# A projection by W.T in seven half-width products per pair of row blocks, with the right-hand sums of the next layer finished by accumulating DMAs

## The chip, the cores and the metric

The kernel runs on one core of one Trainium2 chip. The time is that of one execution on the device, in microseconds (us), and the median of several executions is compared. A profile of a single execution gives the time of every instruction: PE is TensorE (matmuls), PEld its weight loads, DVE VectorE, ACT ScalarE, POOL GpSimd, SP SyncE.

## The reference

There are N = 4096 nodes with D = 512 features. `adj` is a 4096 x 4096 matrix, W is 512 x 512, all in float32.

```
# layer 0
inc = adj + (adj > 0) / max(sqrt(row sum of (adj > 0)), EPS)
x1  = layernorm(x + (inc @ x) / (row sum of inc))

# layer 1
A2     = adj + I
dscale = diagonal(A2) ** -0.5
temp   = A2 @ x1 @ W.T
out    = layernorm(x1 + relu(dscale[:, None] * A2 * dscale[None, :] @ temp))
```

So layer 1 is two products by A2 (the program calls them k = 2 and k = 3), with a projection by W.T and a scaling of the rows by dscale in between.

## The kernel before, in words

**Strassen's scheme, two levels deep.** A product of two matrices that are cut into four quarters each needs seven products of quarters instead of eight, in Winograd's form, with sums of quarters on the left (S1 to S4), on the right (T1 to T4) and on the result. The kernel does this twice. The outer level cuts A2 and x1 into quarters: its seven products are numbered p = 1 to 7. Each outer product is again cut in four, and its seven inner products run as seven 512-column matmuls per 128 rows of the inner dimension, each into a PSUM bank of its own. The eighth bank, `spare()`, is for everything else.

**The steps.** `steps` lists (k, s, p, kk). For each k the result's columns are handled in two strips, s = 0 and 1, each strip does its outer products p in the order 4, 5, 1, 6, 7, 2, 3 (k = 2) or 2, 3, 5, 1, 6, 7, 4 (k = 3), and each outer product takes eight steps kk = 0 to 7 of seven matmuls (`multiply2`, L250). That makes 224 steps. Layer 0 runs before them in its own loop, with one level of the scheme (L455).

**What VectorE does for a step.** `prepare(n)` (L216) forms the four left-hand sums of step n (`add_up`, L166 to L169); in p = 1 and 2 for kk below 4, and in p = 6 and 3 for kk from 4 on, it also adds a tile of A2 to a resident tile r (L232 and L224, 2048 elements per partition). `sum_b` (L245 to L247) forms the right-hand sums of two steps. Everything is issued in the order of the program text, engine by engine: step n's code first prepares step n + 2, then issues the matmuls of step n, then the rest. The tiles for the sums are three in turn, so `prepare(n + 2)` can begin when TensorE has read the sums of step n - 1.

**What happens after eight steps.** `outer` (L682) combines the seven banks, through `inner` (L661: two copies by ScalarE, seven VectorE instructions of 512 elements), either straight into one of the four result quarters c11, c12, c21, c22 (`into`), or through a tile y that is then added to quarters (`by_way`). What remains to be added between whole quarters is put into the list `deferred`, and each later step takes one entry of it, after its `prepare` and `sum_b` and ahead of its matmuls. For k = 2 the lower half of the result (c21, c22; h = 1) is complete after p = 7, the upper half (c11, c12; h = 0) after p = 3.

**The projection.** When a half of a strip is complete, its eight row blocks of 128 rows are put into `queue`, and steps kk = 1 to 5 take one each, after their own seven matmuls. `project` (L733) multiplies the row block by W.T in four 512-column matmuls that add up in the spare bank (L740); ScalarE scales the rows by dscale on the way out (L743). The right-hand operands of k = 3 lie in DRAM (the tiles `ob`): B11, B21, B22 and the sums T1 to T4. The lower half is written as B21 and B22 (L745). For the upper half the matching lower block is read back (L748), B11 is written (L749), and one step later VectorE forms T1 to T4 in `outer_sums` (L127 to L133) and they are written (L754). In k = 3 SP loads these operands again (L238). The DMAs of the projection are issued on GpSimd's queue (POOL).

The first steps of p = 2 and p = 3 (h = 1), and of p = 4 and p = 5 of the next strip (h = 0; for the last strip, p = 2 and p = 3 of k = 3) are where the projection is interleaved.

Of the kernel before, what the change touches and what calls it, by code (L numbers as in the profile page):

```python
# [26 lines left out]
def tile_adj_resnorm_d2(  # L27
# [56 lines left out]
    small = ctx.enter_context(tc.tile_pool(name="small", bufs=6))  # L84
# [107 lines left out]
    queue, later, deferred = [], [], []  # L192
# [57 lines left out]
    def multiply2(n, acc, between=None):  # L250
        k, s, p, kk = steps[n]
        a, sm = ready.pop(n)
        b, t = (y[n // 2][:, kk % 2] for y in (raw_b, sums_b))
        for m, (right, left) in enumerate((
            (a[:, A11, :], b[:, 0, :]), (a[:, A12, :], b[:, 2, :]), (sm[:, S2, :], t[:, 2, :]),
            (sm[:, S1, :], t[:, 0, :]), (sm[:, S3, :], t[:, 1, :]), (sm[:, S4, :], b[:, 3, :]),
            (a[:, A22, :], t[:, 3, :]),
        )):
            if m == 3 and between is not None:
                between()  # L260
            nc.tensor.matmul(acc[m], left, right, start=(kk == 0), stop=(kk == NQ - 1))  # L261
# [101 lines left out]
    def spread(j, part):  # L363

        if part == 0:
            n = small.tile([P, 2], F32, name="n")
# [104 lines left out]
    def take(h, acc):  # L471

        y = row_tile("z", 4)
# [5 lines left out]
    def combine(acc):  # L479

        q1, q2, q6, q5, q7, q3, q4 = acc
        top, low = row_tile("z", 4), row_tile("z", 4)
        p1, p5 = row_tile("p1", 1)[:, 0:W], row_tile("p5", 1)[:, 0:W]
        u2, u3 = row_tile("u2", 1)[:, 0:H], row_tile("u3", 1)[:, 0:H]
        deg = small.tile([P, 2], F32, name="deg")
# [19 lines left out]
    def layer0(j, C):  # L505

        rd = small.tile([P, 2], F32, name="rd")
# [28 lines left out]
    deg0 = small.tile([P, 2], F32, name="deg")  # L536
# [118 lines left out]
    wt = accs.tile([P, ND, D], F32, name="wt")  # L655
# [26 lines left out]
    def outer(k, p, acc):  # L682
# [13 lines left out]
        if k == 2:  # L696
# [6 lines left out]
            elif p == 7:  # L703
                def then(i, y):
                    nc.vector.tensor_sub(c21[:, i, :], c21[:, i, :], y)
                    less(c22[:, i, :], y, c12[:, i, :])
                by_way(then)
            else:
                dst = {2: c11, 3: c12}[p]
                by_way(lambda i, y: add(dst[:, i, :], y))  # L710
# [22 lines left out]
    def project(h, item):  # L733

        j, r, cols = item
        b = j + h * NP
        pv = spare()
        for f in range(2):
            for e in range(2):
                nc.tensor.matmul(pv, C_of[2][h][f][:, 2 * r + e, cols], wt[:, 2 * f + e, :],  # L740
                                 start=(f + e == 0), stop=(f + e == 2))
        z = row_tile("z", 4)
        nc.scalar.activation(z, pv, AF.Copy, scale=dscale[:, b:b + 1])  # L743
        if h:
            nc.gpsimd.dma_start(out=in_outer(3, j, slice(B21, B22 + 1)), in_=split(z))  # L745
            return
        low = split(row_tile("z", 4))
        nc.gpsimd.dma_start(out=low, in_=in_outer(3, j, slice(B21, B22 + 1)))  # L748
        nc.gpsimd.dma_start(out=in_outer(3, j, slice(B11, B11 + 1)), in_=z[:, 0:H].unsqueeze(1))  # L749

        def rest():
            t = row_tile("t", 1, (P, 4, H))
            outer_sums(t, z[:, 0:H], z[:, H:D], low[:, 0, :], low[:, 1, :])
            nc.gpsimd.dma_start(out=in_outer(3, j, slice(T1, T4 + 1)), in_=t)  # L754
        later.append(rest)
# [10 lines left out]
    def fetch(kind, h, *items):  # L766

        for j, _, _ in items if kind is not project else ():
# [80 lines left out]
    for n, (k, s, p, kk) in enumerate(steps):  # L849
# [11 lines left out]
        if deferred:  # L861
            deferred.pop(0)()
        multiply2(n, acc, (lambda: take_up(items.pop(0))) if len(items) > 1 else None)
        if n == 0:
            layer0(NP - 1, C)
        elif n == 1:
            operands(NP - 1, C)
            nc.gpsimd.dma_start(out=wt, in_=w_t.rearrange("(a p) o -> p a o", p=P))
# [4 lines left out]
        for rest in held:  # L873
            rest()
        if 1 <= kk <= (6 if end else 5):
            for kind, args in queue[:2]:
                fetch(kind, *args)
        if kk == NQ - 1:
            outer(k, p, acc)
            if (k, p) in DONE:  # L880
                h = DONE[k, p]
                if n + 1 < len(steps):
                    queue.extend(((project, layer1)[k - 2], (h, b)) for b in blocks(h, s))
# [50 lines left out]
```

## Time and profile before

| | us |
|---|---|
| median of 3 runs | 2297.93 (2297.89 to 2298.2) |
| the profiled execution | 2296.9 |
| its span, first to last instruction | 2295.1 |
| TensorE busy | 2269.1 |
| VectorE busy | 1799.6 |
| ScalarE busy | 349.0 |
| GpSimd busy | 235.0 |

The granted TensorE clock is 0.996 of full speed. The products of k = 2 and 3 begin at about 804 us and last to the end. A line of the profile's groups has the source line, the engine, the operation, the tiles (out<-in), the shape and the count, then the busy time, the mean duration of one in ns, and the idle time of the engine just before the group with what ended it. A line of the chain of waits in order of time has its start, its length, and what ran. A line of the timeline has start, length, engine, line and operation; what stands in brackets at its end is the time the engine was idle before it, and who ended that. A line of the waits has who waited for whom, the sum in us, how often, and the longest. An f32 matmul appears as two records.

### The profile page before, as it was taken

The numbers are of one execution on the slowest core, as the hardware profiler recorded it, in microseconds if no ns is written. First come the engines' busy times: TensorE is split into PE (matmuls) and PEld (weight loads), VectorE is DVE, ScalarE is ACT, GpSimd is POOL, SyncE is SP. The second block draws the span as 40 slices with busy tenths as digits, with TensorE's granted clock in tenths as the row PEclk, the third lists the DMA queues.
The fourth block names the chain that finished last, engine by engine and source line by source line (L and its number), as shares of the span: only waits on it lengthen the run. The fifth ranks groups of instructions, "written<-read, shape, count | busy, mean of one in ns | idle before, by whom it ended". The sixth has DMA issues, their size and how long they took to land.

```text
span 2295.1 us, 20944 instructions
## 1 busy us (share of the span) xinstructions
PE 2269.1 (99%) x7166; PEld 1345.7 (59%) x7167; DVE 1799.6 (78%) x2563; ACT 349.0 (15%) x802; POOL 235.0 (10%) x384
## 2 busy tenths in 40 slices
PE   8999999999999999999999999999999999999997
PEld 6888888888888844444444444444444444444443
DVE  6988898988988777787666778666567788767787
ACT  4333233332231000000000000000000011200013
POOL 0111111211122100000101100010100000100010
PEclk9999999999999999999999999999999999999998
DMA  9788778877776576474665856476665676766672
GB/s 328 276 283 264 253 233 275 271 263 260 250 246 230 205 269 258 187 271 178 241 242 227 299 190 247 161 284 255 236 237 212 227 247 240 261 242 216 222 257 105
DMA packets 149482, 553.64 MB, mean 241 GB/s; under 512 B 16592, under 2 KB 24800, under 8 KB 110976
## 3 DMA queue, kind: packets, MB, share of 16 engines
q1 hardware_dynamic: 114624, 417.38, 51.4%
q0 software_dynamic: 34752, 134.93, 16.5%
q8 instruction: 57, 0.93, 0.2%
q14 instruction: 49, 0.40, 0.0%
HBM read 438.98 MB, written 113.26 MB: 241 GB/s over the span
## 4 chain that ended last, share of the span: by engine, by line
PE 91%; DVE 3%; DMA 3%; issue 2%; ACT 0%; POOL 0%; SPq 0%; ACTq 0%; DVEq 0%; POOLq 0%
PE q L261 56%; PE q L455 27%; PE q L740 5%; PE q L468 2%; DMA nat<-adj 1%; DMA a<-adj_r 1%; PE q L760 1%; DVE s L166 0%; DVE a L425 0%; DMA ob<-t 0%; DVE mask L418 0%; DVE r L232 0%; ACT nat L315 0%; DMA sc<-n 0%; DVE s L168 0%
## 5 line engine op out<-in xcount | busy, mean ns | idle before, releaser
L261 PE MATMUL q<-s,ts 128*128 128x512 f32 x1344 | 614.0, 592 | 0.3 <-DVE u L667 0.2
L455 PE MATMUL q<-b,s 128*128 128x256 f32 (+1 forms) x1920 | 454.4, 379 | 0.0
L261 PEld LDWEIGHTS q<-s,ts 128*128 128x128 f32 x1344 | 255.0, 190 | 321.0 <-issue 293.2
L166 DVE TENSOR_TENSOR s<-a 128x1024 f32<-128x1024 f32 x236 | 288.6, 1223 | 167.9 <-PE q L261 132.9
L455 PEld LDWEIGHTS q<-b,s 128*128 128x128 f32 x1920 | 363.1, 189 | 53.1 <-DVE z L493 0.5
L455 PE MATMUL q<-b,a 128*128 128x258 f32 (+1 forms) x1440 | 352.5, 380 | 1.1 <-ACT p L486 1.1
L261 PE MATMUL q<-a,tr 128*128 128x512 f32 x704 | 331.2, 592 | 1.5 <-DMA a<-adj_r 1.4
L455 PEld LDWEIGHTS q<-b,a 128*128 128x128 f32 x1440 | 272.5, 189 | 41.2 <-ACT p L486 1.9
L261 PE MATMUL q<-s,tr 128*128 128x512 f32 x448 | 228.7, 592 | 0.0
L261 PEld LDWEIGHTS q<-a,tr 128*128 128x128 f32 x704 | 131.6, 190 | 158.2 <-issue 153.1
L315 ACT ACTIVATE nat<-nat,tiny 128x512 f32<-128x512 f32 x240 | 170.9, 714 | 239.1 <-DMA nat<-adj 238.9
L261 PE MATMUL q<-a,ts 128*128 128x512 f32 x352 | 180.1, 593 | 0.8 <-DVE y L672 0.8
L169 DVE TENSOR_TENSOR s<-a,s 128x512 f32<-128x512 f32 x236 | 163.3, 692 | 8.0
L168 DVE TENSOR_TENSOR s<-a,s 128x512 f32<-128x512 f32 x236 | 163.2, 692 | 8.1
L418 DVE SCALAR_TENSOR_TENSOR mask<-a,sc 128x1024 f32<-128x1024 f32 (+2 forms) x129 | 154.0, 1195 | 2.1
L425 DVE TENSOR_TENSOR a<-a,mask 128x1024 f32<-128x1024 f32 x123 | 150.7, 1225 | 6.2
L261 PEld LDWEIGHTS q<-s,tr 128*128 128x128 f32 x448 | 85.1, 190 | 107.2 <-issue 100.9
L665 ACT COPY p<-q 128x512 f32<-128x512 f32 x28 | 16.3, 584 | 742.7 <-PE q L261 742.7
L261 PEld LDWEIGHTS q<-a,ts 128*128 128x128 f32 x352 | 66.6, 190 | 85.9 <-issue 77.7
L740 PE MATMUL q<-wt,c 128*128 128x512 f32 x256 | 115.1, 592 | 0.0
L166 DVE TENSOR_TENSOR s<-r 128x1024 f32<-128x1024 f32 x48 | 58.7, 1222 | 57.1 <-PE q L261 51.1
L261 PE MATMUL q<-r,tr 128*128 128x512 f32 x192 | 90.2, 592 | 0.0
(141 smaller groups left out, 1645.1 us busy)
## 6 DMA issues: line engine op xcount, KB each, us to landing
a<-adj_r SPq DMA_DIRECT2D x112, 1024.0 KB, 5.8
a<-oa SPq DMA_DIRECT2D x80, 1024.0 KB, 5.2
nat<-adj SPq DMA_DIRECT2D x240, 256.0 KB, 7.5
a<-adj_q SPq DMA_DIRECT2D x60, 1024.0 KB, 6.3
tr<-ob SPq DMA_DIRECT2D x112, 512.0 KB, 3.9
oa<-sr POOLq DMA_DIRECT2D x64, 512.0 KB, 7.5
oa<-r POOLq DMA_DIRECT2D x32, 1024.0 KB, 6.1
y<-x POOLq DMA_DIRECT2D x64, 256.0 KB, 6.5
```

What stands on the lines that cost most here:

```text
L166: nc.vector.tensor_add(s[:, S3:S1 + 1, :], a[:, A11:A22 + 1, :], a[:, A21, :].unsqueeze(1).to_broadcast([P, 2, w]))
L168: nc.vector.tensor_add(s[:, S2, :], a[:, A11, :], s[:, S1, :])
L169: nc.vector.tensor_add(s[:, S4, :], a[:, A12, :], s[:, S2, :])
L261: nc.tensor.matmul(acc[m], left, right, start=(kk == 0), stop=(kk == NQ - 1))
L315: nc.scalar.activation(y, a, AF.Sign, bias=tiny, scale=2.0 ** 64, accum_out=accum)
L418: nc.vector.scalar_tensor_tensor(m, v, 0.0, s.unsqueeze(1).to_broadcast(list(v.shape)), op0=ALU.is_gt, op1=ALU.mult)
L425: nc.vector.tensor_add(z, z, y)
L455: nc.tensor.matmul(acc[m][:, 0:w], left, b[:, right, 0:w], start=(kk == 0), stop=(kk == NP - 1))
L468: nc.tensor.matmul(y[:, 0:w], left, slots[kk][:, op, 0:w], start=(kk == 0 and left is k1), stop=(kk == NP - 1 and left is k2))
L665: nc.scalar.copy(p1, q1)
L740: nc.tensor.matmul(pv, C_of[2][h][f][:, 2 * r + e, cols], wt[:, 2 * f + e, :], start=(f + e == 0), stop=(f + e == 2))
L760: nc.tensor.transpose(ps[:, at + i * P:at + (i + 1) * P], C_of[3][h][d // 2][:, 2 * r + d % 2, cols], ident)
```

## The change

W.T is kept as seven right-hand operands of 128 x 2 x 256, three of its quarters and the four sums T1 to T4: four DMAs in step 1 load the quarters (the fourth, B12, into the place of T4), and `outer_sums` forms the four sums in step 4. The projection takes two row blocks at a time, r = 0 and 1 of the same n, as the two row halves of a left operand whose two column halves are the two quarters of the result. Seven products of two 256-column matmuls each go through the spare bank, one after the other, spread over three steps: three in kk = 1 (or 4), three in kk = 2 (or 5), one in kk = 3 (or 6), each placed between the seven matmuls of its step, after the first, the third and the fifth. ScalarE copies each product to one half of the tiles p1, p5, u2, u3. VectorE forms the four left-hand sums behind the first step, and combines the seven copies behind the third.

The combined blocks are scaled in place by ScalarE. The lower half (h = 1) writes B21 and B22 and starts T2, T3 and T4 with its own parts; the upper half (h = 0) writes B11 and T1 and adds its parts of T2, T3 and T4 in DRAM by DMAs that accumulate. The lower block is no longer read back, and `outer_sums` is no longer run for these blocks.

After p = 7 of k = 2 the banks are combined straight into c22, and c21 and c22 get their remaining sums by two entries of `deferred` over whole quarters; while pairs are waiting for the projection, a step takes all entries of `deferred`. The list `pairs` takes the place of `queue` for k = 2.

To make room, the pool `small` has 5 buffers instead of 6, the tile z 2 instead of 4 (in layer 0 as well), and the tiles n, deg and rd 2.

```diff
@@ multiply2
-    def multiply2(n, acc, between=None):
+    def multiply2(n, acc, between):
...
-            if m == 3 and between is not None:
-                between()
+            if m in between:
+                between[m]()
             nc.tensor.matmul(acc[m], left, right, start=(kk == 0), stop=(kk == NQ - 1))
@@ -652,7 +652,8 @@
     quarters = [[accs.tile([P, 4, SW], F32, name=f"c{h}{f}") for f in range(2)] for h in range(2)]
 
     C_of = {2: quarters, 3: quarters[::-1]}
-    wt = accs.tile([P, ND, D], F32, name="wt")
+
+    wt = accs.tile([P, 7, 2, H], F32, name="wt")
     pools["turn"] = [ring, ring, ringx, ring]
     scope = ExitStack()
     pools["resident"] = scope.enter_context(tc.tile_pool(name="resident", bufs=1))
@@ -701,10 +702,8 @@
                 deferred.extend((lambda: add(c12, c11), lambda: nc.vector.tensor_sub(c21, c21, c12),
                                  lambda: add(c12, c22)))
             elif p == 7:
-                def then(i, y):
-                    nc.vector.tensor_sub(c21[:, i, :], c21[:, i, :], y)
-                    less(c22[:, i, :], y, c12[:, i, :])
-                by_way(then)
+                into(c22)
+                deferred.extend((lambda: nc.vector.tensor_sub(c21, c21, c22), lambda: less(c22, c22, c12)))
             else:
                 dst = {2: c11, 3: c12}[p]
                 by_way(lambda i, y: add(dst[:, i, :], y))
@@ -730,29 +729,73 @@
 
         return [(r * NQ + s * SB + n, r, slice(n * P, (n + 1) * P)) for n in range(SB) for r in range(2)]
 
-    def project(h, item):
-
-        j, r, cols = item
+    def project(h, s, n):
+
+
+        cols = slice(n * P, (n + 1) * P)
+        a11, a12, a21, a22 = (C_of[2][h][f][:, 2 * r:2 * r + 2, cols] for r in range(2) for f in range(2))
+        places = [t[:, i * H:(i + 1) * H] for t in (row_tile(t, 1) for t in ("p1", "p5", "u2", "u3")) for i in range(2)]
+        q = []
+
+        def product(left, right):
+            def now():
+                ps = spare()[:, 0:H]
+                for e in range(2):
+                    nc.tensor.matmul(ps, left[:, e, :], wt[:, right, e, :], start=(e == 0), stop=(e == 1))
+                q.append(places[len(q)])
+                nc.scalar.copy(q[-1], ps)
+            return now
+
+        yield {1: product(a11, B11), 3: product(a12, B21), 5: product(a22, T4)}
+        s1, s2, s3, s4 = (y[:, 2 * i:2 * i + 2, :] for y in (row_tile("y", 2, (P, 4, P)) for _ in range(2)) for i in range(2))
+        nc.vector.tensor_add(s1, a21, a22)
+        nc.vector.tensor_add(s2, a11, s1)
+        nc.vector.tensor_add(s3, a11, a21)
+        nc.vector.tensor_add(s4, a12, s2)
+        yield
+        yield {1: product(s2, T2), 3: product(s3, T3), 5: product(s1, T1)}
+        yield
+        yield {1: product(s4, B22)}
+        q1, q2, q4, q6, q7, q5, q3 = q
+        z = [row_tile("z", 2) for _ in range(2)]
+        nc.vector.tensor_add(z[0][:, 0:H], q2, q1)
+        nc.vector.tensor_add(q6, q6, q1)
+        nc.vector.tensor_add(q7, q7, q6)
+        nc.vector.tensor_add(q6, q6, q5)
+        nc.vector.tensor_add(z[0][:, H:D], q3, q6)
+        nc.vector.tensor_sub(z[1][:, 0:H], q4, q7)
+        nc.vector.scalar_tensor_tensor(z[1][:, H:D], q7, -1.0, q5, op0=ALU.mult, op1=ALU.subtract)
+        t = row_tile("t", 1, (P, 4, H))
+        for r in range(2):
+            j = r * NQ + s * SB + n
+            leave_operands(h, j, z[r], t[:, 2 * r, :], t[:, 2 * r + 1, :])
+        yield
+
+    def leave_operands(h, j, z, t, m):
+
+
         b = j + h * NP
-        pv = spare()
-        for f in range(2):
-            for e in range(2):
-                nc.tensor.matmul(pv, C_of[2][h][f][:, 2 * r + e, cols], wt[:, 2 * f + e, :],
-                                 start=(f + e == 0), stop=(f + e == 2))
-        z = row_tile("z", 4)
-        nc.scalar.activation(z, pv, AF.Copy, scale=dscale[:, b:b + 1])
+        nc.scalar.activation(z, z, AF.Copy, scale=dscale[:, b:b + 1])
+        first, second = z[:, 0:H], z[:, H:D]
+        nc.vector.tensor_sub(t, first, second)
+
+        def put(op, y, **how):
+            nc.gpsimd.dma_start(out=in_outer(3, j, slice(op, op + 1)), in_=y.unsqueeze(1), **how)
+
         if h:
+            nc.scalar.mul(m, second, -1.0)
             nc.gpsimd.dma_start(out=in_outer(3, j, slice(B21, B22 + 1)), in_=split(z))
-            return
-        low = split(row_tile("z", 4))
-        nc.gpsimd.dma_start(out=low, in_=in_outer(3, j, slice(B21, B22 + 1)))
-        nc.gpsimd.dma_start(out=in_outer(3, j, slice(B11, B11 + 1)), in_=z[:, 0:H].unsqueeze(1))
-
-        def rest():
-            t = row_tile("t", 1, (P, 4, H))
-            outer_sums(t, z[:, 0:H], z[:, H:D], low[:, 0, :], low[:, 1, :])
-            nc.gpsimd.dma_start(out=in_outer(3, j, slice(T1, T4 + 1)), in_=t)
-        later.append(rest)
+            put(T2, m)
+            put(T3, second)
+            put(T4, t)
+        else:
+            nc.vector.tensor_sub(m, second, first)
+            put(B11, first)
+            put(T1, t)
+            nc.scalar.mul(second, second, -1.0)
+            put(T2, m, accum_op=ALU.add)
+            put(T3, second, accum_op=ALU.add)
+            put(T4, m, accum_op=ALU.add)
 
     def turn_back(ps, at, h, r, cols, fs):
 
@@ -858,20 +901,34 @@
         items = [queue.pop(0) for _ in range(min(len(queue), 2 if end else 1))] if 1 <= kk <= (6 if end else 5) else []
         held = later[:]
         later.clear()
-        if deferred:
+        while deferred:
             deferred.pop(0)()
-        multiply2(n, acc, (lambda: take_up(items.pop(0))) if len(items) > 1 else None)
+            if not pairs:
+                break
+        between = {3: lambda: take_up(items.pop(0))} if len(items) > 1 else {}
+        if 1 <= kk <= 6:
+            if kk % 3 == 1:
+                pair = project(*pairs.pop(0)) if pairs else None
+            if pair is not None:
+                between = next(pair)
+        multiply2(n, acc, between)
         if n == 0:
             layer0(NP - 1, C)
         elif n == 1:
             operands(NP - 1, C)
-            nc.gpsimd.dma_start(out=wt, in_=w_t.rearrange("(a p) o -> p a o", p=P))
+            parts = w_t.rearrange("(f e p) (o d) -> f o p e d", e=2, p=P, o=2)
+            for op, (f, o) in {B11: (0, 0), T4: (0, 1), B21: (1, 0), B22: (1, 1)}.items():
+                nc.gpsimd.dma_start(out=wt[:, op], in_=parts[f, o])
+        elif n == 4:
+            outer_sums(wt[:, T1:T4 + 1], wt[:, B11], wt[:, T4], wt[:, B21], wt[:, B22])
         if n % 2 == 1:
             load_b_up_to(n // 2 + 3)
         for item in items:
             take_up(item)
         for rest in held:
             rest()
+        if 1 <= kk <= 6 and pair is not None:
+            next(pair)
         if 1 <= kk <= (6 if end else 5):
             for kind, args in queue[:2]:
                 fetch(kind, *args)
@@ -879,8 +936,10 @@
             outer(k, p, acc)
             if (k, p) in DONE:
                 h = DONE[k, p]
-                if n + 1 < len(steps):
-                    queue.extend(((project, layer1)[k - 2], (h, b)) for b in blocks(h, s))
+                if k == 2:
+                    pairs.extend((h, s, i) for i in range(SB))
+                elif n + 1 < len(steps):
+                    queue.extend((layer1, (h, b)) for b in blocks(h, s))
             if n == len(steps) - 1 - NQ:
                 last = sorted(blocks(1, s), key=lambda b: b[1])
                 queue.extend((layer1_first, (1, *last[i:i + 2])) for i in range(0, len(last), 2))
```

More of the change, by code (lines that the diff above doesn't have):

```diff
@@ L83, in tile_adj_resnorm_d2 @@
     const = ctx.enter_context(tc.tile_pool(name="const", bufs=1))
-    small = ctx.enter_context(tc.tile_pool(name="small", bufs=6))
+    small = ctx.enter_context(tc.tile_pool(name="small", bufs=5))
     psum = ctx.enter_context(tc.tile_pool(name="psum", bufs=1, space=bass.MemoryType.PSUM))
@@ L191, in tile_adj_resnorm_d2 @@
     made = {"a": 0, "s": 0, "load": 0, "load_b": 0}
-    queue, later, deferred = [], [], []
+    queue, pairs, later, deferred = [], [], [], []
     def fresh():
@@ L365, in spread @@
         if part == 0:
-            n = small.tile([P, 2], F32, name="n")
+            n = w1_pool.tile([P, 2], F32, name="n", bufs=2)
             nc.vector.tensor_reduce(n, counts.pop(j), axis=mybir.AxisListType.X, op=ALU.add)
@@ L471, in take @@
     def take(h, acc):
-        y = row_tile("z", 4)
+        y = row_tile("z", 2)
         nc.scalar.copy(y[:, 0:H], acc[0][:, 0:H])
@@ L481, in combine @@
         q1, q2, q6, q5, q7, q3, q4 = acc
-        top, low = row_tile("z", 4), row_tile("z", 4)
+        top, low = row_tile("z", 2), row_tile("z", 2)
         p1, p5 = row_tile("p1", 1)[:, 0:W], row_tile("p5", 1)[:, 0:W]
         u2, u3 = row_tile("u2", 1)[:, 0:H], row_tile("u3", 1)[:, 0:H]
-        deg = small.tile([P, 2], F32, name="deg")
+        deg = small.tile([P, 2], F32, name="deg", bufs=2)
         nc.scalar.copy(p1, q1[:, 0:W])
@@ L505, in layer0 @@
     def layer0(j, C):
-        rd = small.tile([P, 2], F32, name="rd")
+        rd = small.tile([P, 2], F32, name="rd", bufs=2)
         nc.vector.reciprocal(rd, C[2])
@@ L535, in tile_adj_resnorm_d2 @@
     scale[0] = w1_pool.tile([P, 2, P], F32, name="sc")
-    deg0 = small.tile([P, 2], F32, name="deg")
+    deg0 = small.tile([P, 2], F32, name="deg", bufs=2)
     def load_half(h, c):
@@ L766, in fetch @@
     def fetch(kind, h, *items):
-        for j, _, _ in items if kind is not project else ():
+        for j, _, _ in items:
             b = j + h * NP
```

## The prediction

> **What bounds the kernel now.** I read the busy shares first, then the chain in order of time, then the order of VectorE's instructions where the projection begins.
>
> ```profile
> PE 2269.1 (99%) x7166; PEld 1345.7 (59%) x7167; DVE 1799.6 (78%) x2563; ACT 349.0 (15%) x802; POOL 235.0 (10%) x384
> L740 PE MATMUL q<-wt,c 128*128 128x512 f32 x256 | 115.1, 592 | 0.0
> DVE t L127 <- DMA ob<-t: 64.9, 12, 8.0
> ```
>
> TensorE is busy 99% of the span, and before L740 it never waits. VectorE waits 64.9 us for the T DMA (third line), yet TensorE waits for nothing then: that idle time costs nothing. Matmul records overlap (a mean of 592 ns for half of an f32 matmul), so I take durations from the chain, which is in order:
>
> ```profile
> 59.49 13.87 PE q L468 x64
> ...
> 1068.01 3.43 PE q L740 x8
> 1071.44 6.01 PE q L261 x14
> ```
>
> One step of seven 512-column matmuls takes 6.01 us, 0.858 each; one projected row block (four such) 3.43 us; 32 matmuls of 256 and 258 columns 13.87 us, 0.433 each. So TensorE work saved is time saved, as long as VectorE keeps up. Whether it does is seen at the hand-over from p=7 to p=2 (s=0):
>
> ```profile
> 1044.45 0.68 DVE L666 TENSOR_TENSOR y<-q,p 128x512 f32<-128x512 f32 x1
> ...
> 1045.96 1.88 PE L261 MATMUL q<-a,tr 128*128 128x512 f32 x4
> ...
> 1051.43 1.12 PE L261 MATMUL q<-a,ts 128*128 128x512 f32 x2 [0.16 <-DVE y L672]
> ...
> 1054.55 1.22 DVE L166 TENSOR_TENSOR s<-a 128x1024 f32<-128x1024 f32 x1
> ...
> 1057.14 2.28 DVE L232 TENSOR_TENSOR r<-r,a 128x2048 f32<-128x2048 f32 x1
> ...
> 1058.40 3.60 PE L740 MATMUL q<-wt,c 128*128 128x512 f32 x8
> ...
> 1059.34 0.68 DVE L245 TENSOR_TENSOR ts<-tr 128x512 f32<-128x512 f32 x1
> ...
> 1060.86 1.22 DVE L166 TENSOR_TENSOR s<-a 128x1024 f32<-128x1024 f32 x1
> ```
>
> TensorE starts p=2 at 1045.96 while VectorE works without a gap until past 1060: it combines p=7's banks from 1044.45 to 1054.55, then prepares. TensorE lives on two prepared steps. Start to start, VectorE's pieces cost: a `prepare` 2.59 us, its add to r 2.20, the right-hand sums 1.52. A combination straight into a quarter costs 4.78:
>
> ```profile
> 1293.97 0.68 DVE L666 TENSOR_TENSOR c<-q,p 128x512 f32<-128x512 f32 x1
> ...
> 1298.75 1.22 DVE L166 TENSOR_TENSOR s<-a 128x1024 f32<-128x1024 f32 x1
> ```
>
> [...]
>
> **The change, part by part.**
>
> *Products.* Two row blocks cost 2 × 3.43 = 6.87 us before. Seven products are 14 matmuls of 256 columns: 14 × 0.433 = 6.07. Sixteen pairs: 109.9 − 97.1 = **−12.8 us**. It would be nothing if such a matmul took 0.49. Between two products lie two 512-column matmuls, 1.72 us; the copy out of the bank needs 0.37 (ScalarE's 256-column copy in the layer-0 rows), so one bank is enough.
>
> *The hand-over, p=7 to p=2.* The combination no longer changes c21 and c22 on the way; two whole-quarter instructions do it afterwards, queued on VectorE behind the `prepare` of kk=2 and the sums. Both must end before the first products, which now stand after the first matmul of kk=1 and no longer behind all seven. VectorE: 1044.45 + 4.78 + 2.59 + 2.20 + 1.52 + 2.28 (a 2048-element add) = 1057.82 for c21, 1060.1 for c22. TensorE: kk=0 lasts until 1051.97, the first matmul of kk=1 until 1052.83; then it must wait for c21 and start again (0.16, as above), until 1057.98: 5.15 us. The second product waits 0.13 for c22. Behind that VectorE has prepare and r of kk=3 (until 1064.84) and the pair's sums; the second is ready at 1065.72, TensorE asks at 1065.42: 0.46 with the restart. Together 5.74. The wait at 1051.43 goes (0.42, against a steady 6.01): +5.3. In s=1 the combination starts at 1437.56, and I place TensorE's start at 1438.64: 6.17, less 0.86 saved, +5.3. **+10.6 us**.
>
> *VectorE in p=2 and p=3 of k=2 (h=1).* A pair costs four sums (1.48, as L127 to L133 take 1.47), then seven adds, the scaling on ScalarE and an add behind each scaling: 2.73 plus two chained scalings (0.75 estimated, between L743's 0.69 and L161's 0.81), the negation of m between (0.4) and a last add: 4.6. From the release that lets the seventh prepare of p=2 run to the second sum of the fourth pair (p=3, kk=5) VectorE never rests: seven prepares 18.1, three adds to r 6.6, four right-hand sums 6.1, p=2's combination by way 7.7, two pairs' endings 9.2, three and a half half-pairs' sums 2.5 with the restart: 50.2. TensorE needs 0.86 + 6.44 + 2 × 6.01 + 2 × 7.31 + 6.44 + 7.31 + 0.86 = 48.55 (kk with three products 7.31, with one 6.44). So it waits 1.65, in both s: **+3.3 us**, bounds 0 and 7 (an error of 0.5 in each ending makes 1.0 per s, of 2% in the rest as much). Queued behind these adds is every later `prepare`, so nothing is made up within the group. At the end of p=2 the next banks come free 0.6 us before they are asked for: nothing.
>
> *h=0 pairs* (p=4, p=5, and p=2, p=3 of k=3). VectorE has no adds to r there; an ending is 5.9 with two more adds. It fits between the releases: 0, bounds 0 and 3.
>
> *DMAs.* Per pair 8 (h=1) or 10 (h=0) of 128 or 256 KB on POOL's queue, before 2 or 6; POOL is 10% busy and an issue takes 0.55 to 0.72. No engine but VectorE waits for them: z and t have only room for one pair, so the next pair's ending needs the last DMA landed. It has some 16 us; ten issues take 6, a plain 128 KB DMA lands in 5.4 at the median: hidden. An accumulating one is not shown. Bounds: as the plain one, or the 12.7 of the slowest store into ob. I take about 8, within the 16. A gain from it is excluded, since TensorE waits for no DMA there now. SP's loads of the operands come more than 15 us after the last store: 0.
>
> *Layer 0 with two z buffers:* the next combination comes 20 us after the last store is issued (539.88 against 560.25): 0. *W's four loads and its T sums* (2.8 us of VectorE near 842) shift prepares that are some 2 us early: 0 to 1. *`small` with 5 buffers, deferred in a loop elsewhere:* 0.
>
> Sum: −12.8 + 10.6 + 3.3 = +1.1. The profiled execution took 2296.9 (span 2295.1), 1.0 below the median of the runs, 2297.93. So 2298.0 for its like and **2299.0** for the median.
>
> **Rivals.**
> *The accumulating DMAs are late (slower).* At p=4 to p=5 VectorE starts the combination at most 1 us ahead of need. If a DMA takes 12.7 and only eight are under way at once, the tenth lands after 1.2 + 12.7 + 12.7 = 26.6, 10 later than allowed; TensorE then loses some 9 in each of p=4 and p=5, less in k=3: 2299 + 18 = 2317. It decides from 8 us per DMA on. For it: the slowest store; against: the median.
> *VectorE's endings are dearer (slower).* With 6.0 instead of 4.6 the lag in p=3 grows by 2.8 per s and p=2's bank slack is gone: some 6 more, 2305. For it: the chain between VectorE and ScalarE, twice per ending, is not shown; against: DVE's wait for ACT z at L127 is short (L743's end to L127's start 0.03).
> *The hand-over is hidden (faster).* If VectorE were a step earlier, the 10.6 would go: 2288. Against: the start at 1044.45 follows work without a gap from the release on, in both s.
> *256-column matmuls between 512-column ones cost more*, say 0.49: no gain, 2312. Against: L455 keeps 0.434 over 1232 matmuls.
>
> **How the numbers follow.** A measurement can tell about 0.2%, 4.6 us, from no change: 2293.3 to 2302.5. My forecast's own range is 2295 to 2303; 0.50. Dearer endings 0.20, late DMAs 0.12, the matmul case 0.04: slower 0.36. Hidden hand-over 0.14, in part at least. The range for 8 in 10 leaves out the DMA and matmul cases and a hand-over that is wholly hidden: 2292 to 2309.
>
> **What would show it.** L744 at 0.43 a matmul and some 97 us in all; waits of TensorE for c21's subtraction, twice, 5 us each, after the first matmul of p=2's kk=1; waits of 1 to 3 us for y in p=3's kk=5; no wait of DVE on ob DMAs beyond a few us. No wait at the hand-over, or VectorE waiting on ob for tens of us, would prove me wrong.

## The result, and the profile after

The changed kernel took 2304.97 us at the median of 10 executions (2301.77 to 2307.82). The kernel before, run beside it, took 2300.91 us at the median of 10 (2297.89 to 2302.57). The medians differ by 4.1 us; the ratio is 1.0020, with a 95% interval of 1.0011 to 1.0029, which is slower by some 4.6 us, just at the edge of what can be told from no change. The forecast was 2299.0 us, in a range of 2292 to 2309: +1.1 us. The result lies in that range, and outside the narrower one of 2295 to 2303.

The small sum hides large terms. First the page after, with the engines' busy times and the groups of the new line L744 (line, engine, operation, tiles, shape and count, then busy time, mean ns, idle time before and what ended it):

```profile
PE 2261.5 (98%) x7359; PEld 1384.0 (60%) x7359; DVE 1860.6 (81%) x2715; ACT 403.6 (18%) x946; POOL 291.5 (13%) x467
L744 PE MATMUL q<-wt,y 128*128 128x256 f32 x256 | 65.7, 379 | 0.0
L744 PE MATMUL q<-wt,c 128*128 128x256 f32 x192 | 51.7, 393 | 12.8 <-DVE c L706 12.8
```

TensorE has less to do than before: 2261.5 us. But its products with c as the left operand waited 12.8 us for VectorE's L706, the subtraction that makes c21. The longest waits of TensorE in k = 2 and 3 (who waited for whom, sum, times, longest):

```profile
PE q L744 <- DVE c L706: 12.8, 2, 6.4
PE q L261 <- DVE c L667: 3.6, 3, 3.0
PE q L803 <- DVE c L726: 3.3, 3, 1.3
```

The third wait was there before as well (3.1 us). The second is new: 3.0 us at once, at the change from p = 5 to p = 1 in s = 1. The chain of waits at the hand-over from p = 7 to p = 2 (s = 0), in order of time (start, length, what):

```profile
1044.37 2.28 DVE r L232
1046.65 0.60 DVE c L667
...
1051.43 1.15 DVE s L166
...
1054.02 2.20 DVE r L232
1056.22 0.61 DVE ts L245
...
1057.74 2.21 DVE c L706
1059.95 0.04 issue
1060.00 2.08 PE q L744 x4
1062.07 3.41 PE q L261 x4
1065.49 1.16 PE q L744 x4
```

Two things are to be seen. The subtraction of c21 comes last of a long row on VectorE, in which two adds to r (L232) of 2.28 and 2.20 us stand, those of kk=1 and kk=2 of p=2. And after the wait the matmuls are slow: four of L261 take 3.41 us, 0.85 a record, where 0.43 is the rule. The busy times by stretch say why; the column ahead of the DMA share is the granted TensorE clock:

```profile
1046.00:1053.00 7.00, 6.72 (x17) 2.76 (x15) 6.65 (x10) 0.00 (x0) 0.00 (x0) 1.00 0.59 224
1053.00:1060.00 7.00, 0.58 (x3) 0.00 (x1) 6.86 (x8) 0.00 (x0) 0.00 (x0) 0.69 0.41 151
1060.00:1063.00 3.00, 3.00 (x6) 2.13 (x7) 3.00 (x2) 0.37 (x1) 0.00 (x0) 0.50 0.01 3
1063.00:1066.00 3.00, 3.00 (x5) 1.36 (x5) 2.93 (x4) 0.00 (x0) 0.00 (x0) 0.51 0.00 0
1066.00:1069.00 3.00, 3.00 (x11) 1.89 (x11) 2.49 (x5) 0.37 (x1) 0.00 (x0) 1.00 0.00 0
```

TensorE stands still for 6.4 us, and for some 6 us after that its clock is half. PE counts as fully busy in those 6 us, so the busy shares don't show the loss.

To add the losses up, I take every matmul record of k = 2 and 3 and count what its distance to the next exceeds 0.429 us (512 columns) or 0.216 us (256 columns). I call that the excess; it holds waits and slow stretches alike. The last 16 records of the program, of 128 columns, are not in it.

| excess, us | before | after |
|---|---|---|
| p=7 to p=2, s=0 | 0.4 | 10.2 |
| p=7 to p=2, s=1 | 1.3 | 9.9 |
| p=5 to p=1, s=1 | 0.4 | 5.0 |
| k=2 and 3 in all | 4.3 | 27.1 |

So 22.8 us more is lost. The length of k = 2 and 3, from the first matmul of L261 to the last matmul of all, went from 1479.2 to 1487.6 us, 8.4 more. The last 16 records took 1.2 us less than before, which leaves 13.2 us for what the products save; the forecast was 12.8. The spans of the profiled executions differ by 9.7 (2304.8 against 2295.1). Layer 0 took 788.1 us in the profile before and 788.4 after, and 786.6 to 791.6 over all the profiles. This scatter is larger than the difference of the medians, so below I quote the length of k = 2 and 3, taken from one profiled execution of each kernel, beside the medians.

### The profile page after: what moved, and what is told of

Read it like the earlier page. It is cut to its first block, busy times and chain, and to the rows that moved or that the text cites. A ratio compares the mean times of both kernels' runs of the same rounds, so it can differ in the third digit from the quotient of the medians.

```text
span 2304.8 us, 21997 instructions
## 1 busy us (share of the span) xinstructions
PE 2261.5 (98%) x7359; PEld 1384.0 (60%) x7359; DVE 1860.6 (81%) x2715; ACT 403.6 (18%) x946; POOL 291.5 (13%) x467
## 4 chain that ended last, share of the span: by engine, by line
PE 94%; DVE 3%; DMA 2%; issue 0%; ACT 0%; SPq 0%; ACTq 0%; DVEq 0%
PE q L261 56%; PE q L455 31%; PE q L744 4%; PE q L468 2%; DMA a<-adj_r 1%; DVE r L232 1%; PE q L803 1%; DMA nat<-adj 0%; DVE s L166 0%; DMA s<-adj_q 0%; DMA a<-adj_q 0%; DVE s L168 0%; DVE c L706 0%; ACT nat L315 0%; DVE st L868 0%
## 5 line engine op out<-in xcount | busy, mean ns | idle before, releaser
L261 PE MATMUL q<-s,ts 128*128 128x512 f32 x1344 | 622.3, 595 | 0.1
L261 PEld LDWEIGHTS q<-s,ts 128*128 128x128 f32 x1344 | 256.3, 191 | 308.9 <-issue 281.0
L261 PE MATMUL q<-a,tr 128*128 128x512 f32 x704 | 338.8, 596 | 4.9 <-DVE c L667 3.6
L261 PE MATMUL q<-s,tr 128*128 128x512 f32 x448 | 228.8, 592 | 0.0
L261 PEld LDWEIGHTS q<-a,tr 128*128 128x128 f32 x704 | 132.1, 191 | 149.7 <-issue 136.2
L261 PE MATMUL q<-a,ts 128*128 128x512 f32 x352 | 179.8, 592 | 0.0
L261 PEld LDWEIGHTS q<-s,tr 128*128 128x128 f32 x448 | 85.1, 190 | 93.5 <-issue 83.7
L261 PEld LDWEIGHTS q<-a,ts 128*128 128x128 f32 x352 | 66.8, 190 | 84.4 <-issue 77.7
L408 POOL DMA_DIRECT2D oa<-sr x64 | 57.9, 904 | 283.7 <-DVE sr L399 181.4
L261 PE MATMUL q<-r,tr 128*128 128x512 f32 x192 | 93.2, 592 | 0.0
```

The costliest lines, as they stand in the source:

```text
L408: nc.gpsimd.dma_start(out=dst, in_=sr.rearrange("p m (k i) -> p (m k) i", i=P))
```

## The experiments

### The kernel before, a second time

There is no edit; it is the same kernel on the chip of the next three.

> The kernel before, unchanged, for its trace beside the others of this call. Two readings of the hand-over from p=7 to p=2: if VectorE's wait of 2.0 us for the load of p=2's second tile (seen in the trace after, in both strips) belongs to the chip or the day, it is here too, and the combination of p=7's banks starts some 2 us later against TensorE than in the trace of before, with TensorE waiting 1.5 to 3 us in each strip for the seventh bank. If it belongs to the change, VectorE waits 0 to 0.9 us for it here, as before. Time 2298 to 2301.

It took 2297.37 us; k = 2 and 3 took 1477.0 us with an excess of 3.4, against 1479.2 and 4.3 in the first profile. So a length can be relied on to about 2 us. VectorE did not wait for the load of p=2, kk=1, where the changed kernel had waited 2.0 us in s=0 and 2.1 in s=1. But the three changed kernels that follow, profiled on the same chip, waited 0 to 0.9 us for it too, so this run does not tie that wait to the change.

### Seven fillers in place of the wait

```diff
+                for _ in range(fill):
+                    nc.tensor.matmul(spare(), ident, wt[:, B11].rearrange("p e d -> p (e d)"), start=True, stop=True)
...
-        yield {1: product(a11, B11), 3: product(a12, B21), 5: product(a22, T4)}
+        yield {1: product(a11, B11, 7 if h and n == 0 else 0), 3: product(a12, B21), 5: product(a22, T4)}
```

> The changed kernel with seven 512-column matmuls (6.0 us, results not used) put into the spare bank in front of the first product of the lower half, in both strips, where TensorE waits 6.6 us for c21. Theory one (the wait also halves TensorE's clock: after it, ten to fifteen matmuls ran at half rate, 3.0 to 3.2 us more in each strip): TensorE doesn't idle, the clock stays at 1.0, the wait becomes work of the same length, and the time falls by about 6 us against the changed kernel: 2299 where that is 2305. Rival (those microseconds are further waits for VectorE and not the clock): the same time as the changed kernel within 1 us, or up to 1 us more.

2303.53 us (17 executions), ratio 1.0025 (1.0018 to 1.0032); k = 2 and 3: 1485.6 us, 2.0 less than after, where theory one gave 6. No stretch of half clock followed the hand-over. But a filler stood 1.18 us from the next, not 0.86, so seven lasted until 1063.2, 2.9 us past c21's end at 1060.34. The run shows the clock, not the saving; that was left to four fillers, below.

### c21 and c22 by way of y again

```diff
-                into(c22)
-                deferred.extend((lambda: nc.vector.tensor_sub(c21, c21, c22), lambda: less(c22, c22, c12)))
+                def then(i, y):
+                    nc.vector.tensor_sub(c21[:, i, :], c21[:, i, :], y)
+                    less(c22[:, i, :], y, c12[:, i, :])
+                by_way(then)
```

> The changed kernel with the sums of c21 and c22 formed on the way again, bank by bank, as in the kernel before; all else of the change stays. Theory one (what costs is that the two whole-quarter sums stand behind a prepare, its add to r and the right-hand sums): c21 is ready with the combination, 10.1 us after its start and not 13.4; TensorE waits about 2 us for the seventh bank and 1 to 2 for c21 in place of 6.6[...]; 6 to 7 us less per strip, so about 2292 where the changed kernel has 2305. Rival (VectorE's volume up to the pair's sums decides, whatever the order): the wait only moves to the sums y in kk=2, and the time falls by 1 to 3 us.

2303.2 us (11 executions), ratio 1.0022 (1.0013 to 1.0031). The first waits of this run:

```profile
PE q L746 <- DVE y L754: 9.3, 2, 4.7
PE q L805 <- DVE c L728: 3.3, 3, 1.3
```

The wait for c21 is gone, and one for the pair's sums y, one step later, stands in its place in each strip, 4.8 us of excess with half clock behind it. k = 2 and 3 took 1483.9 us. That is the rival's account, and not theory one's.

### The deferred sums, c21 and c22, ahead of the next step's work

```diff
         load_up_to(n + LA + PF)
+        while pairs and deferred:
+            deferred.pop(0)()
         if n + LA < len(steps):
...
-        while deferred:
-            deferred.pop(0)()
-            if not pairs:
-                break
+        if deferred:
+            deferred.pop(0)()
```

> The changed kernel with the two whole-quarter sums ahead of the prepare in p=2's first step, instead of behind it, its add to r and the right-hand sums. Same volume of work, another order. Theory one (only the order costs): no wait for c21 any more, 2305 falls by 15 to 20 us to about 2287. Rival (VectorE's volume decides): c21 is in time, but the second sum of the pair's left operands stays where it was, about 21.3 us after the combination starts, and TensorE, now earlier, waits for it in kk=2 for 5 to 6 us, with the clock halved after it: within 3 us of the changed kernel.

2300.55 us (21 executions), ratio 1.0012 (1.0006 to 1.0019); k = 2 and 3: 1482.1 us. Its first wait:

```profile
PE q L744 <- DVE y L752: 9.7, 2, 5.3
```

c21 was in time, and again y was late, by as much as before. These two runs say that the order within VectorE's row only moves the wait: between the last product of p=7 and the first pair's sums there is more work on VectorE than TensorE gives it time for. An add to r still stood ahead of the pair's sums in both: what is moved ahead here are the entries of `deferred`.

### Adds to r two steps later

The add to r of step n had been issued in `prepare(n)`, two steps before TensorE reads that step. It is moved behind the pair's work of step n.

```diff
-        if k == 2 and p in (1, 2) and kk < EARLY:
-            nc.vector.tensor_add(r, r, a)
         ready[n] = a, sm
...
+        a_now = ready[n][0]
         multiply2(n, acc, between)
...
             next(pair)
+        if k == 2 and p in (1, 2) and kk < EARLY:
+            add(resident[kk], a_now)
```

> The adds to r of the first two strips of p=1 and p=2 (k=2, kk under 4) are issued two steps later, when their block is used, and after the pair's work of that step; nothing else differs from the changed kernel. Theory A (the VectorE work ahead of a new first use sets both waits: the combination of p=5 starts late because the pair's ending and two adds to r stand before it, and in p=2 an add to r stands before the sums): the wait of about 3.2 us at p=5 to p=1 and its stretch of half clock vanish (excess there from 5.0 to under 1 us); the hand-over of p=7 to p=2 shortens by the 1.3 us of an add to r at most, since the wait for c21 is not behind it. About 5 us under the changed kernel, some 2299 to 2300 us. Theory B (the wait at p=5 to p=1 comes from the bank's reading alone, whatever stands before it): no change, 2304 us. Theory C (the adds are only moved to where they delay the next use): a new wait of 2 to 3 us elsewhere, 2303 to 2305 us.

2288.87 us (5 executions), ratio to the kernel before 0.9964 (0.9952 to 0.9977): faster than both. The gain over the changed kernel is far above what I expected: 16.7 us in k = 2 and 3 (1471.0), some 13 by the ratios. I had allowed 1.3 us at the hand-over. The timeline of TensorE there (start, length, engine, line, operation; in brackets the idle time before) shows why:

```profile
1051.94 1.02 PE L259 MATMUL q<-a,tr 128*128 128x512 f32 x2
1054.26 1.13 PE L742 MATMUL q<-wt,c 128*128 128x256 f32 x4 [1.30 <-DVE c L704]
1055.22 1.02 PE L259 MATMUL q<-a,tr 128*128 128x512 f32 x2
```

Two adds to r stood between TensorE's last steps and c21, not one: that of kk=1 delayed the combination, that of kk=2 the subtraction. (That of kk=0 stood further ahead, before VectorE's wait for a load.) Without them the wait is 1.30 us, and the two matmul records after it span 1.02 us as always: no slow stretch follows this wait. The excess fell from 10.2 and 9.9 to some 1.5 in each strip, and the one at p=5 to p=1 went altogether. A smaller one came up at the end of p=1, at 1337 us: a wait of 1.87 us, then six records in 4.37 us instead of 2.74. There VectorE had first waited 3.87 us for a load of p=1 (until 1328.51), and then worked without a gap into the combination. In the runs below that have p=1's adds late it waited 3.7 us at that place, in the changed kernel 2.15. An add that comes later keeps its tile of A2 longer; that this delays the load is likely, but has not been tried.

```profile
1336.17 1.02 PE L259 MATMUL q<-r,tr 128*128 128x512 f32 x2
1339.06 1.23 PE L259 MATMUL q<-r,tr 128*128 128x512 f32 x2 [1.87 <-DVE c L665]
1340.09 4.37 PE L259 MATMUL q<-s,ts 128*128 128x512 f32 x6
```

### Sums first, and c21 and c22 by slices

```diff
-                deferred.extend((lambda: nc.vector.tensor_sub(c21, c21, c22), lambda: less(c22, c22, c12)))
+                deferred.append(lambda: complete(0))
...
+    def complete(n):
+        (_, c12), (c21, c22) = (tuple(t[:, :, n * P:(n + 1) * P] for t in half) for half in quarters)
+        nc.vector.tensor_sub(c21, c21, c22)
+        less(c22, c22, c12)
...
             next(pair)
+            if kk % 3 == 0 and pairs and pairs[0][0]:
+                complete(pairs[0][2])
```

The entries of `deferred` are taken ahead of the next step's work, as in the run with the sums first. (The expectation says of the pair's sums that they are made ahead of the adds to r; only the deferred sums are, the pair's own follow.)

> The pair's sums are made ahead of the adds to r, and of c21 minus c22 and of c22's new value only the columns of the coming pair are made at the hand-over; the other two thirds follow before each later pair. Theory A (VectorE's amount of work between the last product of p=7 and the sums of the first pair decides): 3.2 us less work ahead of the sums than in the run with the sums first, so the wait of 5.3 us for the sums falls to about 2.1 us in each strip, with a shorter or no stretch of half clock: 6 to 12 us less than the run with the sums first, some 2290 to 2294 us; the wait at p=5 to p=1 stays at about 3 us. Theory B (the waits cost nothing by themselves, and the changed kernel is slower by its instructions alone): within 2 us of the run with the sums first.

2294.16 us (13 executions), ratio 0.9983 (0.9974 to 0.9992): at the upper end of what Theory A gave, 6.4 us under the median of the run with the sums first, and k = 2 and 3 took 1476.2 us against 1482.1 there. The waits for the sums:

```profile
PE q L750 <- DVE y L758: 4.2, 2, 2.6
PE q L261 <- DVE c L667: 3.0, 1, 3.0
```

9.7 us have become 4.2. In s = 0 the excess of 2.8 still had a slow stretch behind it, in s = 1 that of 1.7 had none. A slice cost 0.69 us twice, against 2.28 and 2.29 us for the whole quarters: the 3.2 us less that were expected.

### Both

The edits of the runs with the adds late and with the slices, in one kernel:

```diff
-        if k == 2 and p in (1, 2) and kk < EARLY:
-            nc.vector.tensor_add(r, r, a)
...
+        while pairs and deferred:
+            deferred.pop(0)()
...
+            if kk % 3 == 0 and pairs and pairs[0][0]:
+                complete(pairs[0][2])
+        if k == 2 and p in (1, 2) and kk < EARLY:
+            add(resident[kk], a_now)
```

> Both edits together: sums first, c21 and c22 by slices, and the adds to r late. Theory A (the three waits with their stretches of lower clock are all that the change costs beside its products, which save 12.8 us): the waits at p=7 to p=2 fall under 1.5 us each and that at p=5 to p=1 vanishes, so the part of k=2 and k=3 is some 20 us shorter than in the changed kernel and 10 to 13 us shorter than in the kernel before: 2284 to 2290 us. Theory B (something else that the change brought, such as its DMAs or the number of matmuls, takes the saving): not under 2296 us even with the waits gone.

2286.22 us (5 executions), ratio 0.9951 (0.9939 to 0.9964): within 2284 to 2290, the fastest kernel of this study. k = 2 and 3 took 1467.1 us, 12 less than before and 20.5 less than after. The first waits of TensorE in that part:

```profile
PE q L807 <- DVE c L724: 3.3, 3, 1.3
PE q L259 <- DVE c L665: 1.2, 2, 0.6
PE q L748 <- DVE c L733: 1.2, 2, 0.6
```

None is longer than 1.3 us, and no matmul runs at half clock but the last ones of the program, as in the first profile of the kernel before. The excess is 5.3 us, 1.0 more than before, so the length differs from that of before by −13.1 us beside it: what the products were to save.

### The accumulating DMAs made plain

```diff
-            put(T2, m, accum_op=ALU.add)
-            put(T3, second, accum_op=ALU.add)
-            put(T4, m, accum_op=ALU.add)
+            put(T2, m)
+            put(T3, second)
+            put(T4, m)
```

> The three DMAs of the upper half that add into T2 to T4 write instead; the kernel leaves out that addition, all else is the same. If accumulating DMAs cost the kernel time (their landing delays a tile or a later load): 3 us or more less than the changed kernel. If they lie beside other work: within 2 us of it, with the same waits of TensorE at p=7 to p=2 and p=5 to p=1; the landing of these DMAs alone would then be shorter than the median of 6.7 to 7.1 us.

The kernel leaves out the addition into T2, T3 and T4. 2303.21 us (one execution, which can't tell a few us); k = 2 and 3 took 1484.0 us, 3.6 less than after. TensorE's waits are at the same places, and the excess is 23.1 us, 4.1 less than after, mostly in one hand-over; so what is shorter is the waits, not the rest. The DMA issues (tiles, engine, count, KB each, median us to landing), first of the changed kernel, then of this one:

```profile
ob<-t POOLq DMA_DIRECT2D x80, 128.0 KB, 6.7
ob<-z POOLq DMA_DIRECT2D x64, 128.0 KB, 7.1
```

```profile
ob<-t POOLq DMA_DIRECT2D x80, 128.0 KB, 5.3
ob<-z POOLq DMA_DIRECT2D x64, 128.0 KB, 5.8
```

These groups mix both kinds, and their medians fall by 1.3 to 1.4 us. Taken by themselves, the 48 accumulating DMAs landed 8.4 us after their issue at the median (12.1 at most), and the same 48 made plain 5.8 (8.7 at most). VectorE waited for no such DMA in k = 2 and 3 of either kernel. The accumulation is hidden. This run tells something else: in s = 1 VectorE did not wait for the load of kk=1, and the wait for c21 was 5.04 us; in s = 0, where it did wait (1.5 us), it was 6.58. Whether the plain DMAs have to do with that, one execution does not show.

### Four fillers

```diff
-        yield {1: product(a11, B11, 7 if h and n == 0 else 0), 3: product(a12, B21), 5: product(a22, T4)}
+        yield {1: product(a11, B11, 4 if h and n == 0 else 0), 3: product(a12, B21), 5: product(a22, T4)}
```

> As the run with seven filler matmuls, but with four, at the hand-over of p=7 to p=2 in both strips. A filler took 1.18 us there (two 0.43 us pieces and a new weight), so four last 4.7 us and end before c21 is ready. Theory A (the lower TensorE clock after the wait costs 3.1 us of each hand-over's 10 us): the wait of 6.6 us for c21 stays, now partly filled, the matmuls after it are 0.43 us apart, and k=2 with k=3 is about 6 us shorter than in the changed kernel (1487.6 us); about 2298 to 2300 us. Theory B (the 0.85 us spacing after the wait comes from something other than idleness, such as late operands): the spacing stays at 0.85 us and the time within 2 us of the changed kernel.

2299.38 us (21 executions), ratio 1.0002 (0.9995 to 1.0009); k = 2 and 3: 1481.4 us, 6.2 less than after, as Theory A had it. The timeline of TensorE at the hand-over:

```profile
1053.97 4.57 PE L743 MATMUL q<-wt,ident 128*128 128x512 f32 x8
1060.65 1.10 PE L746 MATMUL q<-wt,c 128*128 128x256 f32 x4 [2.10 <-DVE c L706]
1061.59 1.02 PE L261 MATMUL q<-a,tr 128*128 128x512 f32 x2
```

and the stretches of the same times as above:

```profile
1053.00:1060.00 7.00, 5.37 (x11) 1.46 (x9) 6.86 (x8) 0.00 (x0) 0.00 (x0) 1.00 0.43 150
1060.00:1063.00 3.00, 2.35 (x8) 1.54 (x9) 2.96 (x3) 0.37 (x1) 0.00 (x0) 1.00 0.01 3
```

Here c21 is as late as ever (the product starts at 1060.65), yet the clock stays at 1.00 and two records span 1.02 us. Matmuls whose result nobody reads made this part 6 us shorter, and the kernel some 4 us faster by the ratios. That separates the two parts of the loss in the changed kernel: of 9.6 and 9.3 us of a hand-over in the two strips, 6.6 are the wait and 3.0 and 2.7 the clock, 5.7 together. That 6.2 came so near to it is in part luck: in s = 1 VectorE had no load to wait for, and c21 came some 1.4 us sooner, while the last 16 records took 1.2 us more than after.

### One set of adds at a time

```diff
+        if k == 2 and p == 1 and kk < EARLY:
+            nc.vector.tensor_add(r, r, a)
         ready[n] = a, sm
...
+        if k == 2 and p == 2 and kk < EARLY:
+            add(resident[kk], a_now)
```

(in place of the two `p in (1, 2)` of the run with both; the other run has p = 1 and 2 exchanged)

Only p = 2 late:

> Only the adds to r of p=2 are issued two steps later; those of p=1 stay as in the changed kernel. If the gain of the run with both comes from the two adds to r that stand before c21 at p=7 to p=2: the excess there falls from 10 us to about 1.5 us per strip with no stretch of half clock, the wait of 3.2 us at p=5 to p=1 and its half clock stay (5.0 us), and no new wait follows later in p=1: k=2 with k=3 1470 to 1472 us, some 2288 to 2290 us. If the two sets of adds depend on each other: over 2292 us.

2290.65 us (5 executions), ratio 0.9968 (0.9956 to 0.9981); k = 2 and 3: 1474.1 us. That is 13.5 us less than after, not the 16 to 18 of the forecast: in s = 1 VectorE waited 3.9 us for the load of kk=1, TensorE then 2.4 us for c21, with a slow stretch behind it. s = 0 had the 1.5 us expected.

Only p = 1 late:

> Only the adds to r of p=1 are issued two steps later; those of p=2 stay. The wait at p=5 to p=1 vanishes (5.0 us with its half clock), the hand-overs of p=7 to p=2 keep their 10 us each. If VectorE is then late at the end of p=1 as in the run with both, 3.7 us of it come back there (a wait of 2.0 us and its half clock) and the time is within 3 us of the changed kernel; if not, it is 5 us shorter, about 2299 us.

2300.49 us (21 executions), ratio 1.0014 (1.0008 to 1.0021); k = 2 and 3: 1482.0 us, 5.6 less than after. The wait at p=5 to p=1 went, and one of 2.3 us came up at the end of p=1, this time with no slow stretch; the hand-overs of p=7 to p=2 kept their 6.1 and 6.6 us of waiting. So the larger part of the gain comes from the adds of p = 2. The two sets are not independent to the microsecond, since each run also has other waits for loads.

### All together

The length of k = 2 and 3 without its excess and without the last 16 records, for the kernels that add no matmuls:

| | length, us | excess, us | last 16, us | what is left, us |
|---|---|---|---|---|
| before, first profile | 1479.2 | 4.3 | 6.8 | 1468.1 |
| before, second profile | 1477.0 | 3.4 | 5.6 | 1468.0 |
| after | 1487.6 | 27.1 | 5.6 | 1454.9 |
| by way of y | 1483.9 | 22.2 | 6.8 | 1454.9 |
| sums first | 1482.1 | 20.4 | 6.8 | 1454.9 |
| adds late | 1471.0 | 9.2 | 6.8 | 1455.0 |
| slices | 1476.2 | 14.5 | 6.8 | 1454.9 |
| both | 1467.1 | 5.3 | 6.8 | 1455.0 |
| plain DMAs | 1484.0 | 23.1 | 6.1 | 1454.8 |
| p=2's adds late | 1474.1 | 12.8 | 6.4 | 1454.9 |
| p=1's adds late | 1482.0 | 20.5 | 6.6 | 1454.9 |

The last column falls by 13.1 to 13.2 us with the change and is then the same in all variants to about 0.1 us. What distinguishes them is only the waits and the slow stretches.

## Why the forecast came out as it did, point by point

**Near in the sum, for partly wrong reasons.** The forecast of −12.8 + 10.6 + 3.3 = +1.1 became −13.2 + 18.4 + 0 + 4.6 = about +10 in the profiled execution (+8.4 in the length of k = 2 and 3, whose last records took 1.2 less), and about +4.6 by the ratio. One term was foretold that did not come, and two came larger than foretold. That the first made up for a part of the other two is luck.

*Products: right.* A record of 256 columns stands 0.216 us from the next, 0.43 a matmul; the table gives −13.1 to −13.2 for the forecast's −12.8.

*Hand-over: the mechanism right, the size too small.* L706 is waited for at the place and twice, as foretold, but an average of 9.2 us more was lost per strip than before, not 5.3. The wait was forecast at 5.15: it was 6.58 where VectorE had first waited 1.5 to 2.1 us for the load of p=2's kk=1, 6.10 after a wait of 1.0, and 5.04 in the one strip where it hadn't. In the changed kernel:

```profile
1041.77 1.23 DVE L166 TENSOR_TENSOR s<-a 128x1024 f32<-128x1024 f32 x1 [2.04 <-DMA a<-adj_r]
```

From the combination's start to c21's end took 13.4 us, as in the forecast's row of VectorE (1044.45 to 1057.82). The row was therefore right, and it had no term for that load. Both strips of the profiled execution have this wait (2.0 and 2.1 us), those of the variants 0 to 3.9, those of the kernel before 0 to 0.9. Three changed kernels have no more than the kernel before, as said above, so the change alone does not bring it; why the load is late has not been tried, and is open. The other missing term is the clock: 3.0 and 2.7 us in the two strips. The forecast's restart of 0.16 us treated TensorE as running at once at its full speed.

Here the forecast could have been better with what was to hand. The profile of before has such a stretch at its end: after three waits of 1.1 to 1.4 us, close together, the clock is 0.50 from 2280 us on, and the last 13 records of L760 take 3.04 us. (In the changed kernel, whose clock stayed at 1.00 after the same three waits, these 13 take 1.64.) With that in the profile, a forecast wait of over 5 us was reason for a term for the clock. At the hand-over 6.4 us of idleness were followed by some 6 us at a clock of 0.50.

*VectorE's lag in p=3, kk=5 (+3.3): it did not occur.* The sums of the fourth pair were ready 2 us before TensorE asked. The step that failed is TensorE's side of that ledger, "0.86 + 6.44 + 2 × 6.01 + 2 × 7.31 + 6.44 + 7.31 + 0.86". A product is two 256-column matmuls, 0.86 us, as the forecast itself counts them in *Products*; there a step with three products is 6.01 + 3 × 0.86 = 8.59 us and one with one product 6.87, where the ledger has 7.31 and 6.44. TensorE's side was 4.7 us too short. VectorE's side was near: 51.3 us measured for 50.2, an ending 4.54 for 4.6.

*Pairs of h=0 at nothing: wrong in one place, +4.6.* The ending was 5.73 us, as estimated (5.9). But in p=5, kk=6 of s=1 it stands right ahead of the prepare for p=1, whose kk=0 and 1 bring adds to r; the forecast said "VectorE has no adds to r there" and looked at p=4 and p=5 only, not at what the last pair pushes into p=1. VectorE's row there, from the ending's last instruction to the combination:

```profile
1294.96 0.42 DVE L792 TENSOR_TENSOR t<-z 128x256 f32<-128x256 f32 x1
1295.29 1.22 DVE L166 TENSOR_TENSOR s<-a 128x1024 f32<-128x1024 f32 x1
...
1297.88 2.28 DVE L232 TENSOR_TENSOR r<-r,a 128x2048 f32<-128x2048 f32 x1
1300.08 0.68 DVE L667 TENSOR_TENSOR c<-q,p 128x512 f32<-128x512 f32 x1
```

The combination of p=5 started at 1300.08, and TensorE waited 3.18 us for a bank and lost 1.8 more at half clock. Bounds of 0 and 3 were given: the wait reached the upper one and the clock was beyond it. The run with p=1's adds late removes this wait, which shows the cause.

*DMAs: right that they are hidden.* VectorE waited for none of them. The forecast took about 8 us for an accumulating DMA: 8.4 was measured, 2.6 more than for a plain one. The rival was to decide from 8 us on; it did not come about at 8.4, so that bound was too low. (The rival supposed that only eight are under way at once: in the profile after, never more than eight DMAs of POOL's queue were between issue and landing.)

**Rivals.** Late accumulating DMAs: refuted, as VectorE waited for none, and what is left in the table is the same with plain ones. Dearer endings: refuted, 4.54. 256-column matmuls at 0.49: refuted. The hidden hand-over did not come about by itself; with sums first, slices and late adds the kernel took 2286.2, near the forecast's 2288, which still held the 3.3 us that did not come.

## What to carry to other kernels

In these runs a single stall of an almost saturated TensorE mostly cost more than its length once it passed about 2 us (ten of thirteen from 2.0 to 3.2 us and all ten from 4.5 us up, by 1.6 to 3.1 us), and the slow stretch of matmuls after it is part of its price; the busy shares do not show that (3.00 us busy of 3.00 at a clock of 0.50). When work moves in front of a consumer, list everything on the feeding engine between the last release and that first use, and ask of each whether it must stand there; here adds of 2.3 us each, needed much later, cost about as much as the whole change could save. And take durations in a ledger from one place for both sides: the same product counted once as 0.87 and once as 0.43 us made a wait that did not exist.

## What the runs showed of the hardware

**Waits and the clock.** In all the profiles of k = 2 and 3, taking the waits at the hand-overs, each as the excess of the record ahead of it: after none of the waits under 2.0 us did the records stand further apart; of thirteen from 2.0 to 3.2 us ten were followed by a slow stretch and three (3.18, 2.28 and, behind the four fillers, 2.27 us) were not; after all ten from 4.5 us up there was one. A stretch cost 1.6 to 3.1 us more, mostly 1.8 after the shorter waits. Away from the hand-overs, waits for a load near the start of k = 2 were followed by no slow stretch, the longest 2.36 us. At the very end of the program three waits of 1.1 to 1.4 us stand close together, and in 11 of 13 profiles half clock followed them (a clock of 0.50 from 2280 us on in the profile before); so short waits are not free of it when they come in a row.

Why a wait of 3.18 us passed once without a slow stretch and was followed by one seven times, no run here tries.

**Fillers.** One filler stood 1.18 us from the next, where two records of 0.43 us make 0.86. The trace of TensorE's weight loads shows why:

```profile
1053.98 0.19 PEld L743 LDWEIGHTS q<-wt,ident 128*128 128x128 f32 x1 [0.24 <-issue]
1055.05 0.30 PEld L743 LDWEIGHTS q<-wt,ident 128*128 128x128 f32 x2 [0.89 <-PE q L743]
1056.24 0.30 PEld L743 LDWEIGHTS q<-wt,ident 128*128 128x128 f32 x2 [0.89 <-PE q L743]
```

The load of the next filler waited 0.89 us for the filler ahead of it, which writes the same bank (every filler takes `spare()` anew). It is not the load as such: every matmul record of the kernel has one (7359 of each in the profile after), and the records of L261 stand 0.43 us apart all the same. The expectation of the run with four fillers speaks of a new weight; the weight is the same each time.
